# Turning the first norm's result in 32 by 32 blocks on VectorE, with tokens in another order, instead of on TensorE

## The chip, the cores and the metric

One core of a Trainium2 chip. The metric is the device time of one execution of the whole program, in microseconds (us). The engines are named as the profile names them: PE (TensorE), DVE (VectorE), ACT (ScalarE), POOL (GpSimd) and SP (SyncE, which here only issues DMAs).

## What is computed

One decoder layer over 16 sequences of 512 tokens with 256 features, float32 throughout. Cut to what matters here:

```python
x = layernorm(x + attention(x))      # 16 heads of 16, causal, rope, LoRA on q and v
x = layernorm(x + ffn(x))            # first norm's result goes into the FFN
# ffn: h = gelu(butterfly(x @ W_exp + b_exp) + up_bias)      1024 hidden units
#      y = butterfly(h) @ W_con + b_con + down_bias
```

Both butterflies are linear and are folded into the two weight matrices at the start of the program, so that the FFN is two matrix products with a gelu between them. The first, the expansion, needs the first norm's result with features on the partitions; the norm makes it with tokens on the partitions. So each sequence's 512 by 256 result has to be turned.

## The kernel before

**Slots.** The program is an order written out by hand. A sequence is 20 slots long (`per`), four quads of 5 slots each (two feature chunks by two head parities). In each slot PE makes one share of the score products twice: once for the row maxima of the present quad (`largest`, L407, tile `pa` in most slots) and once for the softmax weights of the quad three quads, 15 slots, behind (`weights`, L457, tile `pb`). DVE reads the first for the maxima (L426, `junk`), ACT takes the exponential of the second (L488), POOL zeroes the masked half of the diagonal blocks (L492). `pa` and `pb` are one buffer each, so that the scores of a slot wait until DVE and ACT have read those of the slot before. Then `weigh` (L506) multiplies the weights with v (`po`, L516), and after it come the tasks of the slot's list `others[s]`, in the order of their `add` calls, and last those of `holes[s]`. Each engine takes its own instructions in this order; SP does so with the DMAs, and a DMA that has to wait holds all DMAs behind it on SP.

**The tail of a sequence.** The numbers below count slots from the sequence's first; slot 40 + n is slot n of the sequence two later, so that these tasks are the fillers between that sequence's score products. In slots 40 to 42 the attention's output is projected and added to x in tile `z` (L589, L601), `spread`, `offset` and `centre` (L616, L628, L635) make the first norm in place on `z`, the last of them on ACT in slot 44. In slot 45 `turn_x1` (L647) runs for both feature chunks: four PE transposes of 128 by 128 each into a PSUM bank, one DVE copy of the bank into `x1T` (L653); POOL then adds the output bias to `z` (L657). In slots 46 to 49 `hidden` (L664) makes the expansion's eight chunks of 128 hidden units, two in a slot (`ph`; a chunk is 8 products in the code, two feature halves by four column groups of 32, and 16 matmuls in the profile), and DVE or ACT copies each out (L680, L682). In slot 50 ACT applies the gelu. From slot 51 `contract` (L691) makes the second product (`py`, L81 in `columns`), one token tile of 128 in two halves, each half one task; the last token tile's halves stand in slots 63 and 64, which are slots 43 and 44 of the next sequence. `spread`, `offset`, `centre` and `store` make the second norm in slots 65 to 68.

**Other tasks there.** `project_v` (L380) of the sequence two later has one of its four tiles in slot 42. The heads' scales take a chain of their own through SP: `normalize_heads` (L533) stores the sums and moves the odd rows (L546, L550) in slot 45, `gather` (L554) loads the sums as `few`, DVE inverts them (`invert`, L561), SP stores them (`recips`), repeats them (`wide`) and loads them (`spread`), and POOL multiplies with them in slots 49 and 50 (`scale`, L577).

The last two sequences have an order of their own: sequence 14's turn stands in slot 46, its expansion from slot 47 on, one chunk in a slot; sequence 15 is turned at the very end. A pool of three PSUM banks, `ps_w`, serves `ph`, `py`, `pvv`, `pwo` and `pt`.

Of the kernel before, what the change touches and what calls it, by code (L numbers as in the profile page):

```python
# [11 lines left out]
F32 = mybir.dt.float32  # L12
BF16 = mybir.dt.bfloat16
AF = mybir.ActivationFunctionType
ALU = mybir.AluOpType
PSUM = bass.MemoryType.PSUM

P = 128
NH = 16
DH = 16  # L20
HG = 32
NG = P // HG
# [11 lines left out]
def decoder_layer(  # L34
# [18 lines left out]
    nc = tc.nc  # L53
    B, T, D = x.shape
    NT = T // P
    NC = D // P
    DHID = wcon.shape[0]
    NHC = DHID // P
# [5 lines left out]
    ring2 = ctx.enter_context(tc.tile_pool(name="ring2", bufs=2))  # L64
# [3 lines left out]
    dram = ctx.enter_context(tc.tile_pool(name="dram", bufs=4, space=bass.MemoryType.DRAM))  # L68
# [5 lines left out]
    def bank(name, shape):  # L74
        return ps_w.tile(shape, F32, tag="w", name=name)

    def columns(out, w, moving, start, stop):

        for g in range(NG):
            part = slice(HG * g, HG * (g + 1))  # L80
            nc.tensor.matmul(out[part, :], w[:, part], moving, start=start, stop=stop)  # L81
# [10 lines left out]
    xTs, zs = {}, {}  # L92
# [23 lines left out]
    wdn = const.tile([P, NHC, D], F32, name="wdn")  # L116
    bias2 = const.tile([P, 2, D], F32, name="bias2")
# [337 lines left out]
    state = {}  # L455
# [151 lines left out]
    def stats_of(which, b, t):  # L607
        if t == 0:
            state["stats", which, b] = small.tile(
                [P, NT, 2], F32, tag=f"stats{which}", name=f"stats{which}_{b}"  # L610
            )
        bn = small.tile([P, nc.vector.BN_STATS_DIM], F32, tag="bn", name=f"bn{which}_{b}_{t}")
        nc.vector.bn_stats(bn, zs[b][:, t, :])
        nc.vector.bn_aggr(state["stats", which, b][:, t, :], bn)
# [13 lines left out]
    def offset(which, b, t0=0, t1=NT):  # L628
        stats, norm = state["stats", which, b], state["norm", which, b]
        ts = slice(t0, t1)  # L630
        nc.vector.scalar_tensor_tensor(  # L631
            norm[:, 2, ts], stats[:, ts, 0], -1.0, norm[:, 1, ts], ALU.mult, ALU.mult
        )
# [10 lines left out]
            )  # L644


    def turn_x1(b, c):  # L647
        if c == 0:
            state["x1T", b] = ring2.tile([P, NC, T], F32, tag="x1T", name=f"x1T_{b}", bufs=1)
        pt = bank(f"pt1_{b}_{c}", [P, NT, P])  # L650
        for t in range(NT):
            nc.tensor.transpose(pt[:, t, :], zs[b][:, t, c * P : (c + 1) * P], ident)  # L652
        nc.vector.tensor_copy(  # L653
            state["x1T", b][:, c, :], pt.rearrange("p t q -> p (t q)")
        )
        if c == NC - 1:
            nc.gpsimd.tensor_tensor(  # L657
                zs[b],
                zs[b],
                bias2[:, 0:1, :].to_broadcast([P, NT, D]),  # L660
                ALU.add,
            )

    def hidden(b, hc, fused=False):  # L664
        if hc == 0:
            state["h", b] = hpool.tile([P, NHC, T], F32, tag="h", name=f"h_{b}")
        ph = bank(f"ph_{b}_{hc}", [P, T])
        for c in range(NC):
            columns(
                ph,  # L670
                wup[:, c, hc * P : (hc + 1) * P],
                state["x1T", b][:, c, :],
                c == 0,
                c == NC - 1,
            )
        h = state["h", b][:, hc, :]
        if fused:
            nc.scalar.activation(h, ph, AF.Gelu, bias=hbias[:, hc : hc + 1])  # L678
        elif hc % 4 == 0:
            nc.vector.tensor_copy(h, ph)  # L680
        else:
            nc.scalar.copy(h, ph)  # L682

    def gelus(b, count=NHC):
        h = state["h", b]
        for hc in range(count):
            nc.scalar.activation(  # L687
                h[:, hc, :], h[:, hc, :], AF.Gelu, bias=hbias[:, hc : hc + 1]
            )

    def contract(b, t, half):  # L691
        if half == 0:
            state["py"] = bank(f"py_{b}_{t}", [P, D])
        py = state["py"]
        for hc in range(half * NHC // 2, (half + 1) * NHC // 2):
            columns(
                py,
                state["h", b][:, hc, t * P : (t + 1) * P],
                wdn[:, hc, :],
                hc == 0,  # L700
                hc == NHC - 1,
            )
        if half == 1:
            nc.vector.tensor_add(zs[b][:, t, :], py, zs[b][:, t, :])  # L704
            stats_of(2, b, t)

    def store(b):
        nc.sync.dma_start(out[b].rearrange("(t p) d -> p t d", p=P), zs[b])
# [14 lines left out]
    end = B * per + behind  # L723
# [6 lines left out]
    def add(s, f, *args):  # L730
        others[s].append(lambda: f(*args))

    def start_projection(b, side, c):
        state["pr", b, side, c] = project(b, side, c)
# [13 lines left out]
    for b in range(B):  # L748
        s = b * per
        if b > 0:  # L750

            at = {1: (-16, -11, -13, -9), B - 1: (-3, 2, 10, 10)}.get(b, (-3, -1, 2, 12))
            for t in range(NT):
                add(s + at[t], project_v, b, t)
        if b + 1 < B:

            add(s - head * (b == 0), load_xT, b + 1)
            at = {0: (2, 5, 7, 10), 1: (3, 6, 8, 11)}.get(b, (10, 10, 10, 10))
            for i, (c, side) in enumerate(chains):
                holes.setdefault(s + at[i], []).append(  # L760
                    lambda b=b, side=side, c=c: start_projection(b + 1, side, c)
                )
                turning = s + max(at[0] + 1 + 3 * i, at[i] + 1)
                for step in range(3):
                    add(turning + step, turn, b + 1, side, c, step)
                for step in range(1 + side):
                    add(turning + (6 if i == 3 else 4) + step, part, b + 1, side, c, step)
        add(s + 9, load_x, b)
        add(s + 11, place_largest, b, 0)
        add(s + 21, place_largest, b, 1)  # L770
        for c in range(NC if b + 1 < B else 1):
            if c + 1 < NC:
                add(s + 25 + (b + 1 == B), gather, b, c)
            add(s + (26, 36)[c] + (b + 1 == B), invert, b, c)
            for t in range(NT):
                add(s + ((29, 29, 30, 30), (39, 39, 40, 40))[c][t], scale, b, c, t)
        if b + 1 < B:
            for t in range(NT):
                add(s + (40, 40, 41, 41)[t], project_out, b, t)
                add(s + (40, 40, 41, 42)[t], add_attention, b, t)  # L780
            add(s + 42, spread, 1, b)
            others[s + 43].insert(0, lambda b=b: offset(1, b))
            add(s + 44, centre, 1, b)
            for c in range(NC):
                add(s + 45 + (b + 2 == B), turn_x1, b, c)
        if b + 2 < B:

            late = 2 * (b + 3 == B)
            for hc in range(NHC - late):
                add(s + 46 + hc // 2, hidden, b, hc)  # L790
            holes.setdefault(s + 50, []).insert(0, lambda b=b, late=late: gelus(b, NHC - late))
            for hc in range(NHC - late, NHC):
                holes[s + 50].append(lambda b=b, hc=hc: hidden(b, hc, True))
            for t in range(NT):
                for half in range(2):
                    at = (11, 13, 14, 15, 16, 18, 23, 24)[2 * t + half]
                    if b + 3 == B and t == NT - 1:
                        at = (23, 25)[half]
                    add(s + 40 + at, contract, b, t, half)
            add(s + 65, spread, 2, b)  # L800
            add(s + 67, offset, 2, b)
            add(s + 68, centre, 2, b)
            add(s + 68, store, b)
# [3 lines left out]
    y, z = B - 2, B - 1  # L807
# [4 lines left out]
    for hc, at in ((3, 10), (4, 10), (5, 10), (6, 11), (7, 11)):  # L812
        add(edge + at, hidden, y, hc, True)

    add(end - 3, contract, y, 0, 0)
    add(end - 1, contract, y, 0, 1)
    add(end + 2, contract, y, 1, 0)
    add(end + 2, contract, y, 1, 1)
    for t in range(NT):
        add(end + 2, normalize, z, NC - 1, t)  # L820
    add(end + 2, contract, y, 2, 0)
    for t in range(NT + 1):
        if t < NT:
            add(end + 3, project_out, z, t)
# [2 lines left out]
        if t > 0:  # L827
            add(end + 3, offset, 1, z, t - 1, t)
            add(end + 3, centre, 1, z, t - 1, t)
    add(end + 3, contract, y, 2, 1)  # L830
    add(end + 3, contract, y, 3, 0)
    for c in range(NC):
        add(end + 5, turn_x1, z, c)
    add(end + 5, contract, y, 3, 1)
    for hc in range(NHC):
        add(end + 5, hidden, z, hc, True)
    add(end + 5, spread, 2, y)
# [2 lines left out]
    add(end + 6, store, y)  # L840
    for t in range(NT):
        for half in range(2):
            add(end + 7, contract, z, t, half)
        add(end + 7, finish_tile, z, t)


    first, second = fold_tasks()
# [180 lines left out]
```

## Time and profile before

| what | value |
|---|---|
| device time, median of 3 runs | 1315.29 us (1312.11 to 1317.72) |
| the profiled execution's own time | 1318.97 us |
| its span, first to last instruction | 1317.0 us, so 1.97 us lie around it |
| DVE busy | 780.5 us (59%) |
| ACT busy | 702.9 us (53%) |
| POOL busy | 565.1 us (43%) |
| DVE copies of the turned blocks (L653) | 32, 678 ns each |
| POOL bias add (L657) | 16, 2381 ns each |
| mean share of the 16 DMA engines, by queue | 16.0% and 1.4% for the two that SP and ACT issue to |
| HBM traffic | 40.17 MB read, 18.06 MB written |

A row of the profile that counts a group of instructions reads: line, engine, operation, output from inputs, shape, count, then busy time and the mean duration of one, and after the second bar how long the engine stood idle before them and who ended the wait. Matmuls overlap, so a group's busy time is less than its count times its mean.

### The profile page before, as it was taken

To read this page: it belongs to the slowest core of one execution; us is meant where nothing else is said; L and a number is where in the kernel's file an instruction comes from. 1 tells how busy PE (TensorE), PEld (TensorE's weight loads), DVE (VectorE), ACT (ScalarE), POOL (GpSimd) and SP (SyncE) were. 2 spreads that over 40 slices of the span, in tenths; PEclk is the share of its full clock that TensorE was granted. 3 is DMA by queue.
4 is the path that set the end of the run, shared out by engine and by line. 5 is a ranking of instruction groups with operands and counts; after the bars stand their busy time and mean duration, and the time that the engine had idled before them with its cause. 6 is when DMAs were issued, how large, how long until landed. Compare 5 with 4: busy or idle time off the path is not lost.

```text
span 1317.0 us, 38318 instructions
## 1 busy us (share of the span) xinstructions
PE 1280.6 (97%) x15896; PEld 575.2 (44%) x15896; DVE 780.5 (59%) x2760; ACT 702.9 (53%) x1047; POOL 565.1 (43%) x905
## 2 busy tenths in 40 slices
PE   8888999999999999999999999999999999999998
PEld 3343435444353544435354443535444353444443
DVE  5776746657465665747566574756657474665431
ACT  2574455555646555564655546465555646455643
POOL 4525325445362544536254453625445362532430
PEclk9889999999999999999999999999999999999999
DMA  5411111111212111121211112121211212111101
GB/s 169 132 32 59 40 49 46 56 56 41 82 41 65 47 56 56 41 83 41 69 42 57 56 41 83 41 67 45 56 56 40 83 41 70 41 40 32 43 20 34
DMA packets 64062, 74.07 MB, mean 56 GB/s; under 512 B 23120, under 2 KB 42576, under 8 KB 63888
## 3 DMA queue, kind: packets, MB, share of 16 engines
q1 hardware_dynamic: 60000, 66.07, 16.0%
q10 hardware_dynamic: 3888, 5.55, 1.4%
q8 instruction: 125, 2.05, 0.7%
q14 instruction: 49, 0.40, 0.1%
HBM read 40.17 MB, written 18.06 MB: 44 GB/s over the span
## 4 chain that ended last, share of the span: by engine, by line
PE 92%; DVE 3%; ACT 2%; DMA 1%; issue 1%; POOL 0%; SPq 0%; POOLq 0%; DVEq 0%; ACTq 0%
PE pb L474 21%; PE py L81 17%; PE ph L81 16%; PE po L516 12%; PE pqk L81 8%; PE pa L417 4%; PE pwo L81 4%; PE pvv L81 4%; DVE junk L426 1%; PE pd L81 1%; PE pt L652 1%; PE pa L474 1%; PE pb L417 1%; ACT pT L488 1%; ACT h L687 0%
## 5 line engine op out<-in xcount | busy, mean ns | idle before, releaser
L426 DVE CUSTOM_DVE_ANT_0 junk<-pa,causal 128x384 bf16<-128x384 f32 (+2 forms) x878 | 438.6, 500 | 339.0 <-PE pa L417 271.6
L488 ACT ACTIVATE pT<-pb 128x1024 f32<-128x1024 f32 (+1 forms) x314 | 294.2, 937 | 354.8 <-PE pa L417 183.8
L492 POOL TENSOR_SCALAR_AFFINE_SELECT pT<-pT 128x256 f32<-128x256 f32 x512 | 202.3, 407 | 651.4 <-ACT pT L488 650.4
L474 PE MATMUL pb<-qz,kz 17*128 17x512 f32 (+2 forms) x1756 | 330.9, 475 | 17.6 <-ACT pT L488 11.7
L417 PE MATMUL pa<-kz,qz 32*128 32x384 f32 (+3 forms) x1756 | 330.6, 476 | 3.4 <-DVE mx L426 3.4
L81 PE MATMUL py<-wdn,h 128*32 128x256 f32 x4096 | 244.3, 381 | 0.0
L81 PE MATMUL ph<-x1T,yb 128*32 128x512 f32 x2048 | 231.6, 594 | 0.2 <-ACT h L678 0.2
L474 PEld LDWEIGHTS pb<-qz,kz 17*128 17x128 f32 (+1 forms) x1756 | 142.4, 184 | 196.4 <-issue 92.3
L516 PE MATMUL po<-pT,vaug 128*32 128x512 f32 (+3 forms) x2048 | 180.9, 447 | 1.8 <-POOL pT L492 1.8
L81 PEld LDWEIGHTS py<-wdn,h 128*32 128x32 f32 x4096 | 125.3, 110 | 99.2 <-issue 12.7
L417 PEld LDWEIGHTS pa<-kz,qz 32*128 32x128 f32 (+1 forms) x1756 | 143.2, 185 | 14.6 <-DVE mx L426 11.6
L81 PEld LDWEIGHTS ph<-x1T,yb 128*32 128x32 f32 x2048 | 63.2, 110 | 139.8 <-issue 107.6
L81 PE MATMUL pqk<-xT,wqk 128*32 128x512 f32 x1024 | 117.6, 608 | 0.0
L682 ACT COPY h<-ph 128x512 f32<-128x512 f32 x84 | 49.2, 585 | 117.3 <-PE ph L81 117.2
L516 PEld LDWEIGHTS po<-pT,vaug 128*32 128x32 f32 x2048 | 47.9, 109 | 105.3 <-issue 59.1
L426 DVE DVE_READ_ACCUMULATOR2_ANT mx<- 128x1 f32 x1024 | 84.6, 83 | 0.0
L638 ACT ACTIVATE z<-z,norm 128x256 f32<-128x256 f32 x128 | 66.7, 589 | 23.2 <-DVE norm L631 23.2
L365 POOL TENSOR_TENSOR swap<-swap,rope_sb 128x512 f32<-128x512 f32 x62 | 78.8, 1270 | 0.0
L426 DVE CUSTOM_DVE_ANT_0 junk<-pb,causal 128x256 bf16<-128x256 f32 (+3 forms) x146 | 63.6, 436 | 16.4 <-PE pb L417 2.5
L687 ACT ACTIVATE h<-h,hbias 128x512 f32<-128x512 f32 x113 | 70.8, 709 | 0.2
L704 DVE TENSOR_TENSOR z<-py,z 128x256 f32<-128x256 f32 x64 | 27.2, 425 | 72.9 <-PE py L81 70.6
L81 PE MATMUL pvv<-wv_sb,xT 128*32 128x256 f32 x1024 | 66.5, 379 | 0.0
(91 smaller groups left out, 1192.1 us busy)
## 6 DMA issues: line engine op xcount, KB each, us to landing
xT<-in_xT SPq DMA_DIRECT2D x16, 512.0 KB
swap<-qz SPq DMA_DIRECT2D x64, 128.0 KB
swap<-kz SPq DMA_DIRECT2D x64, 128.0 KB
z<-in_x SPq DMA_DIRECT2D x16, 512.0 KB
wide<-recips SPq DMA_DIRECT2D x31, 256.0 KB
spread<-wide SPq DMA_DIRECT2D x31, 256.0 KB
out_y<-z SPq DMA_DIRECT2D x15, 512.0 KB
x<-x SPq DMA_DIRECT2D x32, 128.0 KB
```

The lines of the kernel that those rows point to most:

```text
L81: nc.tensor.matmul(out[part, :], w[:, part], moving, start=start, stop=stop)
L365: engine.tensor_tensor(swap, swap, rope_sb[:, 1, :], ALU.mult)
L417: lambda i=i, rows=rows, at=at, n=n, t=t, ps=ps: nc.tensor.matmul(ps[:, i, at : at + n], q[rows, par, t * P : n], k_[rows, par, 0:n], star ...
L426: lambda i=i, at=at, n=n, t=t, g=g, ps=ps: nc.vector.tensor_tensor_reduce(out=junk[:, 0:n], in0=ps[:, i, at : at + n], in1=causal[:, T - n ...
L474: lambda i=i, rows=rows, at=at, n=n, k=block, ps=ps: nc.tensor.matmul(ps[:, i, at : at + n], kt[rows, par, k * P : (k + 1) * P], qt[rows, ...
L488: nc.scalar.activation(pT[:, heads, 0:n], ps[:, :, at : at + n], AF.Exp)
L492: nc.gpsimd.affine_select(out=diag, in_=diag, pattern=[[0, 2], [1, P]], compare_op=ALU.is_ge, fill=0.0, base=0, channel_multiplier=-1,)
L516: nc.tensor.matmul(po[HG * g : HG * (g + 1), k * P : T], vaugs[b % 2][:, k, NG * c + g, first : first + HG], pT[:, g, at : at + n], start= ...
L638: nc.scalar.activation(zs[b][:, t, :], zs[b][:, t, :], AF.Identity, bias=norm[:, 2, t : t + 1], scale=norm[:, 1, t : t + 1],)
L682: nc.scalar.copy(h, ph)
L687: nc.scalar.activation(h[:, hc, :], h[:, hc, :], AF.Gelu, bias=hbias[:, hc : hc + 1])
L704: nc.vector.tensor_add(zs[b][:, t, :], py, zs[b][:, t, :])
```

## The change

For sequences 0 to 14 the PE transposes are gone. `turn_blocks`, called in slot 45, turns the four token tiles of `z` on DVE in one instruction, in blocks of 32 by 32: block k of 32 features of all four token tiles comes to lie on 32 partitions each. Four DMAs on SP, one for each group g of 32 partitions, write these to a DRAM tensor `x1rows` (128 KB each, rows of 512 bytes), and a fifth (512 KB, rows of 2 KB) loads `x1T` from it. In `x1T` the tokens then have the order (g, t, i), where token = 128 t + 32 g + i. The order is carried through `hidden` and the gelu, and `contract` undoes it by the columns of `h` that it takes as the stationary operand; sequence 15, which still has `turn_x1`, keeps the plain order. The two DVE copies of a sequence go as well.

Around it: the expansion begins in slot 47 with three chunks in a slot (sequence 13: two, without those that are already fused with the gelu); `project_v`'s third tile moves from slot 42 to slot 46 for sequences 2 to 14; the last token tile's contraction is cut into four quarters in slots 62 to 65 (slots 42 to 45 of the next sequence) instead of two halves in 63 and 64, except for sequence 13; the second norm's `spread` goes from slot 65 to 66, again except for sequence 13. For sequence 14 the turn moves from slot 46 to 45. In the program's order on SP the five new DMAs stand behind the odd rows' move (L550 of the kernel before) and ahead of the load of `few`.

```diff
+    def turn_blocks(b):
+        state["x1T", b] = ring2.tile([P, NC, T], F32, tag="x1T", name=f"x1T_{b}", bufs=1)
+        turned = ring2.tile([P, D // HG, NT, HG], F32, tag="turned", name=f"turned_{b}", bufs=1)
+        nc.vector.transpose(turned, zs[b].rearrange("p t (k j) -> p k t j", j=HG))
+        rows = dram.tile([D, NG, P], F32, tag="x1rows", name=f"x1rows_{b}")
+        for g in range(NG):
+            nc.sync.dma_start(
+                rows.rearrange("(k j) g q -> j k g q", j=HG)[:, :, g, :],
+                turned[HG * g : HG * (g + 1)].rearrange("j k t i -> j k (t i)"),
+            )
+        nc.sync.dma_start(state["x1T", b], rows.rearrange("(c p) g q -> p c (g q)", p=P))
+        nc.gpsimd.tensor_tensor(
+            zs[b],
+            zs[b],
+            bias2[:, 0:1, :].to_broadcast([P, NT, D]),
+            ALU.add,
+        )
...
-    def contract(b, t, half):
+    def contract(b, t, first, past):
...
+            of = h.rearrange("p c (g t i) -> p c t g i", g=NG, i=HG)
+        for hc in range(first, past):
+            for g in range(NG):
+                nc.tensor.matmul(
+                    py[HG * g : HG * (g + 1), :],
+                    of[:, hc, t, g, :],
+                    wdn[:, hc, :],
...
-            at = {1: (-16, -11, -13, -9), B - 1: (-3, 2, 10, 10)}.get(b, (-3, -1, 2, 12))
+            at = {1: (-16, -11, -13, -9), B - 1: (-3, 2, 10, 10)}.get(b, (-3, -1, 6, 12))
...
-            for c in range(NC):
-                add(s + 45 + (b + 2 == B), turn_x1, b, c)
+            add(s + 45, turn_blocks, b)
...
-                add(s + 46 + hc // 2, hidden, b, hc)
+                add(s + 47 + hc // (2 if late else 3), hidden, b, hc)
...
+                for n in range(4):
+                    add(s + 62 + n, contract, b, NT - 1, 2 * n, 2 * n + 2)
+            add(s + 65 + (b + 3 < B), spread, 2, b)
```

More of the change, by code (lines that the diff above doesn't have):

```diff
@@ L689, in gelus, with halves @@
             )
-    def contract(b, t, half):
-        if half == 0:
+    def contract(b, t, first, past):
+        if first == 0:
             state["py"] = bank(f"py_{b}_{t}", [P, D])
         py = state["py"]
[L695 to L703, printed above, removed]
+        h = state["h", b]
+        if b + 1 == B:
+            of = h.rearrange("p c (t g i) -> p c t g i", g=NG, i=HG)
+        else:
+            of = h.rearrange("p c (g t i) -> p c t g i", g=NG, i=HG)
[5 more added lines that the diff above has]
+                    wdn[:, hc, :],
+                    start=(hc == 0),
+                    stop=(hc == NHC - 1),
+                )
+        if past == NHC:
             nc.vector.tensor_add(zs[b][:, t, :], py, zs[b][:, t, :])
             stats_of(2, b, t)
+    def halves(b, t, half):
+        contract(b, t, half * NHC // 2, (half + 1) * NHC // 2)
     def store(b):
@@ L793, in decoder_layer @@
                 holes[s + 50].append(lambda b=b, hc=hc: hidden(b, hc, True))
-            for t in range(NT):
+            for t in range(NT - 1):
                 for half in range(2):
[L796 to L800, printed above, removed]
+                    add(s + 40 + (11, 13, 14, 15, 16, 18)[2 * t + half], halves, b, t, half)
+            if b + 3 == B:
+                for half in range(2):
+                    add(s + (63, 65)[half], halves, b, NT - 1, half)
+            else:
+                for n in range(4):
+                    add(s + 62 + n, contract, b, NT - 1, 2 * n, 2 * n + 2)
+            add(s + 65 + (b + 3 < B), spread, 2, b)
             add(s + 67, offset, 2, b)
@@ L813, in decoder_layer @@
         add(edge + at, hidden, y, hc, True)
[L815 to L818, printed above, removed]
+    add(end - 3, halves, y, 0, 0)
+    add(end - 1, halves, y, 0, 1)
+    add(end + 2, halves, y, 1, 0)
+    add(end + 2, halves, y, 1, 1)
     for t in range(NT):
         add(end + 2, normalize, z, NC - 1, t)
-    add(end + 2, contract, y, 2, 0)
+    add(end + 2, halves, y, 2, 0)
     for t in range(NT + 1):
@@ L829, in decoder_layer @@
             add(end + 3, centre, 1, z, t - 1, t)
-    add(end + 3, contract, y, 2, 1)
-    add(end + 3, contract, y, 3, 0)
+    add(end + 3, halves, y, 2, 1)
+    add(end + 3, halves, y, 3, 0)
     for c in range(NC):
         add(end + 5, turn_x1, z, c)
-    add(end + 5, contract, y, 3, 1)
+    add(end + 5, halves, y, 3, 1)
     for hc in range(NHC):
@@ L842, in decoder_layer @@
         for half in range(2):
-            add(end + 7, contract, z, t, half)
+            add(end + 7, halves, z, t, half)
         add(end + 7, finish_tile, z, t)
```

## The prediction, made before the changed kernel ran

> **What bounds the kernel now.** I read the page first: busy shares, then the chain that ended last, then the rows of what is removed.
>
> ```profile
> PE 1280.6 (97%) x15896; PEld 575.2 (44%) x15896; DVE 780.5 (59%) x2760; ACT 702.9 (53%) x1047; POOL 565.1 (43%) x905
> ...
> PE 92%; DVE 3%; ACT 2%; DMA 1%; issue 1%; POOL 0%; SPq 0%; POOLq 0%; DVEq 0%; ACTq 0%
> ...
> L652 PE MATMUL pt<-ident,z 128*128 128x128 f32 x128 | 17.6, 280 | 0.0
> ```
>
> PE is the bound almost throughout, so a microsecond off PE is worth a microsecond, if nothing else comes late in its place. All 16 turns keep PE busy 17.6 us; 15 go. So the gain has a ceiling of about 15 x 1.1 = 16 us, and the question is whether the replacement arrives in time. For that I read the chain in order of time (start, us, what) over slots 45 to 47 of one sequence in mid-run:
>
> ```profile
> 627.67 0.63 PE pb L474 x2
> ...
> 628.74 0.57 PE po L516 x8
> 629.31 1.02 PE pt L652 x8
> 630.33 0.63 PE pb L474 x2
> ...
> 631.45 3.57 PE ph L81 x32
> 635.02 0.52 PE pb L474 x2
> ...
> 636.10 1.00 PE po L516 x8
> 637.10 3.43 PE ph L81 x32
> 640.53 0.52 PE pb L474 x2
> ```
>
> Slots begin at 627.67, 630.33, 635.02 and 640.53. The turn holds the chain for 1.02 us, and the expansion starts 2.14 us after the turn's start. The products `ph` are the long fillers here: while PE makes them, DVE and ACT catch up on the scores. Next, DVE and SP in the same stretch, from the timeline:
>
> ```profile
> 629.57 0.69 DVE L426 CUSTOM_DVE_ANT_0 junk<-pa,causal 128x512 bf16<-128x512 f32 x1
> ...
> 630.28 1.27 DVE L653 COPY x1T<-pt 128x512 f32<-128x512 f32 x2
> ```
>
> ```profile
> 631.00 0.53 SPq L550 DMA_DIRECT2D x<-x  x1
> 632.08 0.32 SPq L558 DMA_DIRECT2D few<-sums  x1
> 634.35 0.33 SPq L566 DMA_DIRECT2D recips<-few  x1
> 635.81 0.62 SPq L569 DMA_DIRECT2D wide<-recips  x1
> 638.87 0.32 SPq L574 DMA_DIRECT2D spread<-wide  x1
> ```
>
> The two maxima of a slot with 512 columns take DVE about 1.43 us (628.83 to 630.26). SP shows what a trip by way of DRAM costs: `spread` cannot issue until `wide` has landed, 3.06 us after `wide` was issued (256 KB); `recips` to `wide` is 1.46 us (16 KB).
>
> **The change, part by part, for this sequence.**
>
> *Removed.* PE's 1.02 us and DVE's 1.27 us.
>
> *Slots 42 to 45.* Slots 43 and 44 each lose half of a 1.73 us `py` task. Slot 43 gets nothing from it: the scores of slot 44 start at 623.74 because DVE reads slot 43's until 623.67. I charge 1.0 us for that. The other 0.75 us is kept, so slot 45 begins at about 626.9 instead of 627.67. There PE makes scores (1.07), `po` (0.57) and a `py` quarter (0.87), until 629.4. The quarter ends the token tile, so DVE adds it and takes statistics (0.42 + 0.43 + 0.18, with gaps 1.09) until 630.55, and only then turns.
>
> *The DVE turn.* No row has this shape. A turn of 128x32 takes 193 ns (L444); the two copies of 512 columns each (1024 in all) took 1.27 us. Bounds: 0.7 us (a copy of half the columns) and 2.4 us (POOL's pass over 128x1024). I take 1.25 us by the copies, which have its element count. It ends at T = 631.8.
>
> [...]
>
> *The five DMAs.* None is in the trace. Two-part issues of 128 KB (`swap`) follow each other by 0.51 to 0.56 us, so the fourth write is issued at T + 1.7. A 128 KB issue's last packet ended 1.7 us after its start (655.40 to 657.11), and SP goes on 0.37 us after a landing: the load of `x1T` is issued at T + 3.75. The 512 KB load of `xT` ended 3.47 us after issue, that of `z` 3.66 us: T + 7.2, and PE starts at about T + 7.4 = 639.2. From below: issues 0.41 us apart (0.33 as for `rows`), a landing in 1.06 us, the load in 3.3: T + 6.2. From above: the last write as slow as `wide` (3.06) and the load as slow as `z`: T + 8.9.
>
> *When PE wants `x1T`.* Slot 46 now holds only scores and one `pvv` task (0.86 us), until 631.45. Behind the turn on DVE wait slot 46's maxima (631.8 to 633.25), so slot 47's `pa` products wait until 633.25: about 1.35 us of PE idle. POOL's bias add (2.38 us) now follows the turn too, until 634.2, and slot 46's masking (0.41) is behind it: `po` of slot 47 loses another 0.6 us and ends at 635.2. PE then stands at `ph` until 639.2: **4.0 us**.
>
> *What else is behind these waits.* On SP, `few` is issued only after the `x1T` load, and its packets come behind it. DVE waits for `few` at L564 with slot 47's maxima behind it, until about 639.5; `ph` covers that (three chunks, 5.2 us). `spread` lands about 6 us later than now, near 647, while POOL wants it in slot 49, which now begins at about 650: covered, by 3 us; if not, POOL's masks and then `po` wait for the rest.
>
> *Sum.* Slot 47 now ends at 640.53 with four chunks made. After: 639.2 + 7.0 us for four chunks = 646.2. That is **+5.7 us a sequence**: the terms, -1.02 for the turn and +1.0, +1.35, +0.6 and +4.0 for the waits, add to 5.9; I keep the count to slot 47's end. The other chunks and the `py` quarters keep their length. Sequences 0, 13 and 14 have other fillers but the same trip by way of DRAM; I count them alike: 15 x 5.7 = 85 us.
>
> *The clock.* A stretch of nearly 8 us (631.45 to 639.2) would have PE busy for some 1.8 us. What the clock does then, the windows show near the start (stretch, its length, PE, PEld, DVE, ACT, POOL busy, then the granted clock):
>
> ```profile
> 123.20:126.60 3.40, 0.85 (x8) 0.30 (x4) 3.26 (x11) 1.02 (x1) 2.29 (x3) 1.00 0.14 49
> 126.60:133.50 6.90, 6.83 (x52) 3.13 (x52) 2.54 (x12) 3.23 (x7) 2.17 (x4) 0.51 0.01 2
> ...
> 160.80:164.20 3.40, 2.67 (x34) 1.55 (x32) 2.77 (x11) 1.02 (x1) 1.15 (x3) 1.00 0.02 5
> 164.20:167.70 3.50, 3.50 (x24) 1.74 (x28) 2.40 (x9) 3.13 (x6) 0.81 (x2) 0.51 0.00 0
> ```
>
> After 3.4 us with PE 0.85 us busy the clock was halved for 6.9 us, and once for 3.5 us after a much busier stretch. The new stall is as idle as the first of these. Half clock for 3.4 to 6.9 us, part of it still inside the wait, costs 0 to 3.4 us a sequence; I take 1.9: 15 x 1.9 = 28 us.
>
> [...]
>
> **The rivals.**
>
> *Stall without the clock.* The same waits, but the clock holds: 1319 + 85 = 1404, by the median 1400. For it: near 1196 us PE idled 1.4 us at a time and the clock stayed at 1.0. Against it: the first window above.
>
> *Mostly hidden.* The trip takes as little as about 4 us, so that only the DVE and POOL waits stay: (-1.02 + 2.9) x 15 = 28, so 1343. For it: the queue is nearly empty here (41 to 70 GB/s in most slices). Against it: `rows` to the maxima's landing, the smallest such pair, takes 3.75 us without 512 KB to move.
>
> *Not slower.* The mechanism is PE's own lag at slot 47. If the other engines run ahead, so that T comes about 3 us earlier against PE (the turn needs only ACT's `centre`, done at 628.48, and the `py` quarter's statistics) and the writes land quickly, then PE meets `x1T` ready, and 1.02 us a sequence is gained: 1319 - 15 = 1304, by the median 1300. It decides when all waits together stay under 1.02 us. Against it: slots 45 and 46 without long fillers leave PE no lag.
>
> *Worse still.* The late `spread` outlasts its 3 us of cover under a slow trip: 2 to 4 us more a sequence, about 1465.
>
> **How the numbers follow.** Likeliest, at 0.57, is the stall with the halved clock: 1319 + 85 + 28 = 1432 against the profile's own 1319; the median of the runs lies 3.7 us lower, so **1428**. Stall without the clock 0.26, mostly hidden 0.08, not slower 0.04, worse still 0.05. The low end, 1375, is the trip and turn at their lower bounds with the clock held (15 x 4.0 = 60); the high end, 1465, lies 2.5 us a sequence above the forecast, and the upper bounds together would go beyond it. Half a per cent, about 6.6 us, is what a measurement of this kernel can tell from no change: faster 0.04, within it 0.02, slower 0.94.
>
> **What would show it.** In the changed profile, the PE load for `ph` should wait on the DMA `x1T` some 4 us at a time, 15 times; slot 47's `pa` should wait for DVE; the turn should show about 1.25 us; L564's wait for `few` should rise from 13.6 us in all to over 50; PEclk should show digits under 9 in mid-run. If the waits on `x1T` are under 1 us, the DMA step is wrong; if the clock stays at 0.99, the clock step is. I would be wrong outright if PE reached slot 47 later than 635 for a reason that does not lengthen the program.

## The result, and the profile after

The changed kernel takes 1443.05 us in the median of six runs (1440.29 to 1446.99), against 1316.45 us before; the ratio is 1.0971, with a 95% interval of 1.0945 to 1.0997. The forecast was 1428 us in a range of 1375 to 1465. The profiled execution took 1445.02 us, its span is 1443.3 us.

The page of the kernel after: busy shares, the granted clock in tenths, the chain by engine, the expansion's products, and DVE's inversion of `few`.

```profile
PE 1327.3 (92%) x15776; PEld 576.1 (40%) x15776; DVE 790.7 (55%) x2745; ACT 699.3 (48%) x1047; POOL 563.8 (39%) x905
...
PEclk9998999999999999999998989999899999989899
...
PE 76%; DVE 9%; DMA 8%; ACT 3%; issue 2%; SPq 2%; POOL 0%; DVEq 0%; POOLq 0%; ACTq 0%
...
L81 PE MATMUL ph<-x1T,yb 128*32 128x512 f32 x2048 | 258.6, 656 | 61.6 <-DMA x1T<-x1rows 61.4
...
L564 DVE RECIPROCAL few<-few 128x32 f32<-128x32 f32 x31 | 10.9, 353 | 99.3 <-DMA few<-sums 99.2
```

PE's share of the chain fell from 92% to 76%; DVE and the DMAs took what it lost. PE now stands 61.4 us in all for `x1T`. The time in which PE is not busy (span less busy time) grew from 36.4 to 116.0 us, and PE is also busy 46.7 us longer, with 120 matmuls fewer. The clock digits drop to 8 in mid-run; on the page of before they stay at 9 there:

```profile
PEclk9889999999999999999999999999999999999999
```

The chain in order of time for the sequence ahead of the one in the prediction, whose slots are filled alike (slot 45 begins at 591.12 here; start, us, what), shows each link of the trip:

```profile
591.12 0.70 PE pb L474 x2
...
592.94 0.91 PE py L721 x16
...
594.97 1.26 DVE turned L651
...
597.63 2.46 DMA x1rows<-turned
...
600.23 3.60 DMA x1T<-x1rows
...
603.87 7.80 PE ph L81 x48
611.67 0.52 PE pb L474 x2
```

Quarter, statistics, turn, writes, load, expansion: from 592.94 to 603.87 the chain is never on PE's score products. SP in that stretch, from the timeline:

```profile
596.25 1.85 SPq L654 DMA_DIRECT2D x1rows<-turned  x4
600.23 0.38 SPq L658 DMA_DIRECT2D x1T<-x1rows  x1
600.71 0.41 SPq L558 DMA_DIRECT2D few<-sums  x1
604.45 0.33 SPq L566 DMA_DIRECT2D recips<-few  x1
```

The four issues take 1.85 us, SP waits until 600.23 for the writes to land, and only then can `few` go.

The windows around the wait (stretch, its length, PE, PEld, DVE, ACT, POOL busy, then the granted clock, DMA share, GB/s):

```profile
598.60:602.01 3.41, 1.52 (x12) 0.29 (x8) 0.08 (x1) 1.02 (x1) 2.13 (x5) 1.00 0.51 103
602.01:608.84 6.83, 4.97 (x24) 1.17 (x28) 2.71 (x11) 0.00 (x0) 0.00 (x0) 0.50 0.34 107
```

PE was busy 1.52 us of 3.41, then the clock was halved for 6.83 us, 4.97 us of them with PE at work. That is why three expansion chunks took 7.80 us where 5.15 us were due (three times half of the 3.43 us that two took before).

### The profile page after: what moved, and what is told of

It reads as the page before. It is cut to its first block, busy times and chain, and to the rows that moved or that the text cites. A ratio compares the mean times of both kernels' runs of the same rounds, so it can differ in the third digit from the quotient of the medians.

```text
span 1443.3 us, 38171 instructions
## 1 busy us (share of the span) xinstructions
PE 1327.3 (92%) x15776; PEld 576.1 (40%) x15776; DVE 790.7 (55%) x2745; ACT 699.3 (48%) x1047; POOL 563.8 (39%) x905
## 4 chain that ended last, share of the span: by engine, by line
PE 76%; DVE 9%; DMA 8%; ACT 3%; issue 2%; SPq 2%; POOL 0%; DVEq 0%; POOLq 0%; ACTq 0%
PE ph L81 17%; PE pb L474 15%; PE py L721 14%; PE po L516 9%; PE pqk L81 8%; DVE junk L426 4%; PE pa L417 4%; DMA x1T<-x1rows 4%; PE pwo L81 4%; DMA x1rows<-turned 3%; PE pvv L81 3%; SPq L654 1%; ACT pT L488 1%; DVE turned L651 1%; PE pa L474 1%
## 5 line engine op out<-in xcount | busy, mean ns | idle before, releaser
L81 PE MATMUL ph<-x1T,yb 128*32 128x512 f32 x2048 | 258.6, 656 | 61.6 <-DMA x1T<-x1rows 61.4
L721 PE MATMUL py<-wdn,h 128*32 128x256 f32 x4096 | 249.1, 381 | 0.0
L516 PE MATMUL po<-pT,vaug 128*32 128x512 f32 (+3 forms) x2048 | 189.3, 454 | 1.8 <-POOL pT L492 1.8
L81 PEld LDWEIGHTS ph<-x1T,yb 128*32 128x32 f32 x2048 | 67.9, 119 | 230.8 <-issue 147.2
L564 DVE RECIPROCAL few<-few 128x32 f32<-128x32 f32 x31 | 10.9, 353 | 99.3 <-DMA few<-sums 99.2
```

The costliest lines, as they stand in the source:

```text
L516: nc.tensor.matmul(po[HG * g : HG * (g + 1), k * P : T], vaugs[b % 2][:, k, NG * c + g, first : first + HG], pT[:, g, at : at + n], start= ...
L721: nc.tensor.matmul(py[HG * g : HG * (g + 1), :], of[:, hc, t, g, :], wdn[:, hc, :], start=(hc == 0), stop=(hc == NHC - 1),)
```

## The experiments

Every kernel ran next to the kernel before on the same chip. One table first; ratios against the kernel before, with their 95% intervals:

| run | median us | ratio | clock in the profiled run |
|---|---|---|---|
| e1_moves | 1347.07 | 1.0223 (1.0204 to 1.0242) | 0.985 |
| e2_nowait | 1376.24 | 1.0446 (1.0420 to 1.0472) | 0.983 |
| e3_warm | 1425.01 | 1.0818 (1.0780 to 1.0856) | 0.987 |
| e4_turn | 1466.60 | 1.1142 (1.1122 to 1.1161) | 0.942 |
| e5_few | 1448.53 | 1.0995 (1.0966 to 1.1025) | 0.955 |
| e6_nowait_few | 1352.67 | 1.0266 (1.0236 to 1.0296) | 0.989 |
| e7_cover | 1323.45 | 1.0047 (1.0026 to 1.0067) | 0.993 |
| e8_cover_pe | 1329.04 | 1.0078 (1.0052 to 1.0105) | 0.989 |
| e9_few_between | 1319.44 | 1.0007 (0.9989 to 1.0025) | 0.989 |
| e10_early | 1325.68 | 1.0057 (1.0038 to 1.0077) | 0.989 |
| e11_invert | 1315.56 | 0.9980 (0.9963 to 0.9997) | 0.993 |
| e12_shift | 1315.08 | 0.9991 (0.9973 to 1.0009) | 0.994 |

The kernel before has a clock of 0.989 in its profiled run, the changed kernel 0.960.

The theory was the prediction's: waits for `x1T`, small waits for DVE and POOL in slots left without long fillers, and a halved clock (the expectations call its sum of these terms the ledger). The rivals were that the moves are harmless, that DVE's wait for `few` does the damage, and that the clock does not matter.

### The two halves of the change by themselves

**e1_moves**: the turn stays on PE, and with it the plain order of tokens; everything else as in the change.

```diff
-            add(s + 45, turn_blocks, b)
+            for c in range(NC):
+                add(s + 45, turn_x1, b, c)
```

> The moves alone: the turn stays on TensorE (slot 45), the expansion begins in slot 47 and the fillers stand where the change puts them. Theory of the ledger: 1.0 us wait behind slot 43 and about 1.35 us for the maxima behind the DVE copies, a sequence, no trip by way of DRAM and no halved clock: 15 x 2.4 = 35, so about 1350. Rival, the moves cost nothing and all loss is the trip: 1316 to 1322.

Measured 1347, 30 us over the kernel before. The moves have a price of their own with no trip at all. PE's weight loads and matmuls for `pa` wait 23.5 and 7.6 us for DVE's maxima in the profile, against 11.6 and 3.4 us before. That is not all of it: PE is also busy 19.8 us longer (1300.4 us against 1280.6), and by the trace's records the score products, `pa` and `pb` together, cover 418.5 us of the span instead of 402.2. The waits for `pa` before, and then in e1_moves:

```profile
PEld pa L417 <- DVE mx L426: 11.6, 19, 2.1
```

```profile
PEld pa L417 <- DVE mx L426: 23.5, 43, 1.9
```

**e4_turn**: the turn and its trip, all fillers where they were before, `project_v`'s third tile too.

```diff
...
-            add(s + 45, turn_blocks, b)
+            add(s + 45 + (b + 2 == B), turn_blocks, b)
...
-                add(s + 47 + hc // (2 if late else 3), hidden, b, hc)
+                add(s + 46 + hc // 2, hidden, b, hc)
...
+            for t in range(NT):
+                for half in range(2):
+                    at = (11, 13, 14, 15, 16, 18, 23, 24)[2 * t + half]
...
+                    add(s + 40 + at, halves, b, t, half)
```

> The turn alone: block turn and trip, but the expansion from slot 46 and all fillers where they were before. Theory: PE stands at the first expansion chunk in slot 46 for about 7.7 us instead of the several waits, net 7.7 us a sequence and at least as much clock: 15 x 7.7 + 15 x 2.5 = 150, about 1465. Rival, the moves are the larger part of the loss: below 1400.

Measured 1467. The wait for `x1T` is 120.9 us in all, 8.1 us a sequence where 7.7 were expected, and the mean clock falls to 0.942. So the moves of the change are worth their 30 us: the whole loss is 150 us without them and 127 with them.

### The wait, `few`, and the clock

**e2_nowait**: a weight tile in place of `x1T`.

```diff
-                state["x1T", b][:, c, :],
+                (state["x1T", b] if b + 1 == B else wqk)[:, c, :],
```

> The changed kernel, but the expansion of sequences 0 to 14 takes a weight tile of the same shape that lies in SBUF from the start in place of x1T (so it computes something else); the block turn and its five DMAs still run. Theory of the ledger: the 4.0 us wait and the halved clock go, the small waits stay, and DVE's wait for few now shows for up to 0.9 us: 15 x (1.7 to 2.6), 1342 to 1356, clock back at 0.99. Rival, that it is DVE's wait for few, with the maxima queued behind it, that holds PE: above 1400, since that wait is still there.

Measured 1376, above the theory's 1342 to 1356 and below the rival's 1400: neither. The wait for `x1T` and what hangs on it are worth 67 us of the 127, but more was left than I had counted.

**e6_nowait_few**: the same, with `few` loaded ahead of the turn's DMAs.

```diff
-                add(s + 25 + (b + 1 == B), gather, b, c)
+                if b + 1 < B:
+                    others[s + 25].insert(0, lambda b=b, c=c: gather(b, c))
+                else:
+                    add(s + 26, gather, b, c)
```

> As e2_nowait (the expansion of sequences 0 to 14 takes a weight tile in place of x1T), and the load of few ahead of the turn's DMAs. Theory: without the wait for x1T the late few is bare, 0.9 us a sequence; with it gone 15 x 0.9 = 13 less than e2_nowait, about 1363, near e1_moves less the PE turns. Rival, few costs nothing here either: 1376.

Measured 1353: the late `few`, once bare, costs 23.6 us (1376.24 less 1352.67), not 13. That is what the sum for e2_nowait had left out. In e2_nowait DVE waits 97.0 us in all for it, here 16.3. One part of the expectation does not come out: e1_moves less the PE turns would be about 1332, and this run is 20 us above that. PE's loads and matmuls for `pa` wait 38.3 and 16.7 us for DVE's maxima here, against 23.5 and 7.6 us in e1_moves. What of the turn on DVE, the bias add behind it and the five DMAs holds DVE up was not tried apart.

**e5_few**: this order of `few` alone, with the wait for `x1T` left in.

> The changed kernel with one order undone: the load of few stands on SP ahead of the five DMAs of the turn again. DVE's wait for few should fall from 99 us in all to about 15. Theory: PE stands at the expansion for x1T during that wait anyway, so the time stays, 1438 to 1446. Rival, that the late few (and the maxima behind it on DVE) is a cost of its own: 13 us or more less, 1430 or below.

Measured 1449, a little above the expected range, its interval overlapping that of the changed kernel. DVE's wait for `few` is down to 15.1 us, as expected, and PE's wait for `x1T` is about what it was (61.4 us in the changed kernel):

```profile
PE ph L81 <- DMA x1T<-x1rows: 60.0, 15, 7.2
...
DVE few L564 <- DMA few<-sums: 15.1, 12, 9.2
```

The 99 us that DVE stands at `few` in the changed kernel are covered: PE stands for `x1T` at the same time. A long wait in the list of waits cost nothing here, and 23.6 us as soon as the wait above it was gone. With `few` early in both, e5_few and e6_nowait_few differ by the wait for `x1T` alone: the wait and the clock that goes with it are worth 96 us (1448.53 less 1352.67), where the prediction had 15 x 4.0 + 28 = 88.

**e3_warm**: idle products ahead of the first expansion chunk.

```diff
+            if b + 1 < B:
+                fill = bank(f"fill_{b}", [P, D])
+                for n in range(3):
+                    for c in range(NC):
+                        columns(fill, wqk[:, c, n * P : (n + 1) * P], wv_sb[:, c, :], n + c == 0, n + c == 3)
```

> The changed kernel with 2.6 us of idle products on TensorE (48 matmuls of 256 columns on weights, result not used) ahead of the first expansion chunk of sequences 0 to 14, more work for the bound engine. Theory that the stall halves the clock and that this costs 2.1 us a sequence: the products lie inside the 3.7 us wait, the clock stays up, 15 x 2.1 = 32 less, about 1411. Rival, the clock is not driven by this wait or costs nothing: 1443 or, where the products outlast the wait, up to 1460.

Measured 1425: TensorE has 39 us more work to do (15 x 2.6; 32 products of this size took 1.73 us in the kernel before, so 48 take 2.6), and the program is 18 us shorter. The direction is the theory's, the size is 14 us short of it. Its four runs are 1417.64, 1424.38, 1425.63 and 1430.17 us, at mean clocks of 0.987, 0.979, 0.983 and 0.975: by and large the lower the clock, the longer the run, from the first to the last some 10 us for each 0.01. The changed kernel's runs have 0.957 to 0.966. So the products do not keep the clock up in every execution; where they did best, the run is 25 us under the changed kernel's median. What remains of the wait for `x1T` in the profiled run, the first of the four, is 24.1 us on the matmuls, 1.6 us a sequence: the products take 37 us off the wait, about what they add. So what is gained must be the clock's. Counted in that trace's records PE is busy 32 us at half clock, against 89 us in the changed kernel; half of the difference is 28 us, and the run is 27 us shorter than the profiled run of the changed kernel.

### A cover that fits

**e7_cover** puts work that exists anyway into the gap: the projections of a later sequence. Sequences 13 and 14 turn on PE again, and `few` goes first on SP. The cut shows the new places against the kernel before:

```diff
+                early = at if b < 2 else (5, 6, 6, 7)
-                holes.setdefault(s + at[i], []).append(
+                holes.setdefault(s + early[i], []).append(
...
-            late = 2 * (b + 3 == B)
+            late = 2 if b + 3 == B else 4
             for hc in range(NHC - late):
-                add(s + 46 + hc // 2, hidden, b, hc)
+                add(s + (46 if b + 3 == B else 48) + hc // 2, hidden, b, hc)
```

> Another cover for the trip: block turn for sequences 0 to 12 with few first on SP, fillers of before, but the query and key projections of the sequence three later (6.9 us of products) come in slots 45 to 47 instead of 50, and the expansion in slots 48 to 50, its last four chunks fused with the gelu. Theory: x1T lands about when PE gets there, the wait and the halved clock go, and 13 x 1.02 = 13 us of PE turns are gained: 1300 to 1312. Rival, another wait takes its place (the gelus without the projections as cover, the swaps behind the trip on SP, DVE): 1320 to 1350.

Measured 1323, in the rival's range. 120 us of the loss are gone, but not all of it. In its profile PE still waits 7.2 us on the matmuls and 9.3 us on the weight loads for `x1T`, up to 1.6 us at a time: `few`, put first, waits on SP for its own sums and delays the writes. Around 632 us the writes begin 0.97 us after the odd rows' move there, and 0.11 us after it in e9_few_between.

**e8_cover_pe** is the same order with the turn on PE.

> The order of e7_cover with the turn on TensorE, no trip. If the block turn buys the PE time of the turns and nothing else, this is 13 us slower than e7_cover. If the order alone has its price, it shows here against the kernel before: theory 1312 to 1322, rival above 1330.

Measured 1329, between the two ranges: the order alone costs 12 us against the kernel before, and the block turn in it is 5.6 us better than the PE turn (the intervals of the two ratios overlap a little, 1.0026 to 1.0067 against 1.0052 to 1.0105, so that this is not quite clear of the noise), less than the 13 us of PE time that it saves.

**e9_few_between** issues `few` between the four writes and the load of `x1T`.

> e7_cover with the load of few between the four writes and the load of x1T on SP, where SP waits for the writes anyway. In e7_cover SP issued few first and the writes 0.9 us late, and PE stood up to 1.2 to 1.4 us at the expansion. Theory: that wait nearly goes, 13 x 0.9 = 12 less than e7_cover's 1323, about 1312. Rival, the wait is not what separates e7_cover from the kernel before (its gelus without cover are): 1321 to 1324.

Measured 1319, the same as the kernel before: 4 us less than e7_cover where 12 were expected, and below the rival's range too. No wait of PE for `x1T` is left in the list, but its place was taken. The timeline of DVE in e9_few_between:

```profile
639.16 0.35 DVE L564 RECIPROCAL few<-few 128x32 f32<-128x32 f32 x1 [3.97 <-DMA few<-sums]
...
640.57 0.55 DVE L426 CUSTOM_DVE_ANT_0 junk<-pa,causal 128x384 bf16<-128x384 f32 x1
```

DVE stands 3.97 us for `few`, which SP issued at 635.38, right behind the four writes, and slot 47's maxima come after it.

**e11_invert** moves the inversion one slot on.

```diff
-            add(s + (26, 36)[c] + (b + 1 == B), invert, b, c)
+            add(s + (26 + (0 < b < B - 2), 36)[c] + (b + 1 == B), invert, b, c)
```

> e9_few_between with the inversion of few (L564) one slot later for sequences 1 to 13, behind slot 47's maxima on DVE. In e9_few_between the wait for x1T was gone, but DVE stood up to 4.0 us at few, whose load came behind the four writes, and slot 47's maxima and so the scores of slot 48 stood behind it. Theory: with that wait out of the way about 1 us a sequence more is gained, 1303 to 1310, under the kernel before. Rival, the next thing is as late (x1T lands at about the same time, ACT's gelus in slot 50): 1314 to 1320.

Measured 1315.56, ratio 0.9980 (0.9963 to 0.9997): under the kernel before by 0.2%, just clear of its interval, short of the 1303 to 1310 expected and in the rival's range. DVE's and PE's waits there in e9_few_between, and then in e11_invert:

```profile
DVE few L564 <- DMA few<-sums: 45.5, 27, 4.0
...
PEld pa L417 <- DVE mx L426: 15.6, 22, 2.1
```

```profile
PEld pa L417 <- DVE mx L426: 10.9, 16, 2.1
...
DVE few L564 <- DMA few<-sums: 5.0, 12, 1.1
```

DVE's wait fell by 40 us, PE's by 5 and the time by 4: most of DVE's wait had been covered. A short wait of PE for `x1T` is back, 2.8 us on the matmuls and 4.0 on the loads.

**e10_early** and **e12_shift** are two attempts to spread this better: the turn and its writes already in slot 44 with the fourth projection back in slot 50, and the third projection a slot later.

> As e9_few_between, and the block turn with its writes already in slot 44, right behind the centring, the load of x1T in slot 45 as before; the fourth projection goes back to slot 50 behind the gelus, as cover. Theory: x1T lands about 2 us earlier, no wait for it is left and slot 50 loses its gap, so what the PE turns cost is gained: 1300 to 1310. Rival, the turn ahead of slot 45's maxima on DVE holds the scores of slot 46: 1315 to 1325.

> As e11_invert, with the third projection in slot 47 instead of 46, so that DVE's copies spread more evenly over the trip. Theory: within 3 us of e11_invert, since the cover in all is the same. Rival, slot 46 with one filler less lets DVE hold the scores of slot 47: 8 us more or above.

e10_early took 1326, just past the upper end of its rival's range: the turn ahead of slot 45's maxima is no gain. PE's loads for `pa` wait 19.6 us for DVE's maxima, against 15.6 in e9_few_between, which fits the rival, but which of its two moves costs the time was not tried apart. e12_shift took 1315, the same as e11_invert; its ratio is not clear of 1.

## Why the prediction was right, point by point

- **The turn on DVE.** Taken at 1.25 us, measured 1.246 us in the mean of 15 (128x1024, float32; 1.239 to 1.248). The block turn loses in this kernel by the price of its trip (in e4_turn PE waits 8.1 us a sequence for `x1T`) and not by its own time.
- **The trip.** In the sequence shown the turn ends at T = 596.22. The load of `x1T` is issued at T + 4.0 (forecast T + 3.75), PE starts at T + 7.65 (forecast T + 7.4).
- **The wait for `x1T`.** Forecast 4.0 us a sequence, measured 61.4 us over 15, 4.1 us. PE was ready at T + 3.9 in this sequence, 0.5 us later than forecast, so that the two slips nearly cancel: that the wait came out this close is partly luck.
- **The small waits.** Forecast 1.0 + 1.35 us for the moves alone; e1_moves shows 30 us instead of 35. All the terms but the wait for `x1T`, 1.9 us a sequence or 29 us, are what e6_nowait_few has left: 35 us over the kernel before. Slot 45 began 5.1 us before T, against 4.9 forecast.
- **`few`.** It was forecast to be covered, and e5_few shows that it is. Its bare price was set at 0.9 us a sequence in the expectations and is 1.6 us (e6_nowait_few against e2_nowait, 23.6 / 15). The late `spread` was covered too: PE's loads for `po` wait 11.4 us in all behind POOL's product with it, 12.1 us before.
- **The clock.** Forecast 28 us. Counted in the trace's records, PE was busy 89 us at half clock, against 25.5 us before; half of the difference is 32 us. That half of the time is lost fits the sequence shown, where PE was at work for 4.97 us at half clock and the three chunks took 2.65 us longer than due. e3_warm shows that work put into the wait brings 18 us of it back in the median; in its profiled run, the best one, it brings 27 us where the count gives 28. The rest, to 32, is from the trace's count alone. The forecast had the stall as the cause. In eleven sequences the clock was halved during the wait for `x1T` or right after it; in the other four it was halved before that wait began (see the last section), so that there the wait is not what set it off.
- **The sum.** Forecast 113 us, measured 126.6. Of the 13.6 us, about 4 lie in the clock by the trace's count. The other 10 us are 0.6 us a sequence. In the sequence shown, slots 40 to 47 and the fourth chunk take 8.8 us more than before (575.26 to 611.67 and 1.76 us for the chunk, a third of the 5.29 us that slot 48's three take, against 611.20 to 640.53); 2.65 of that is the expansion at half clock, which leaves 6.2 where the ledger had 5.7. This half microsecond is spread over the terms: about 0.15 ahead of slot 45, 0.2 from there to T, 0.25 in the trip, and 0.1 less in the chunks. The last 0.1 us I have not placed. PE is busy longer than the clock and the missing turns explain, by some 31 us over the program. About half of it is there in e1_moves too, where the score products overlap less; that they do so because their pairs wait for DVE is my reading and was not tried.

The rival that ended on the other side needed T about 3 us earlier against PE. e7_cover to e11_invert show the other way to the same end, PE 4 us later with useful work, and what it brings when it is reached: 0.2% at most, where 13 turns take 1.0% on PE. The order takes the rest: by itself it costs 12 us (e8_cover_pe). Against e8_cover_pe, e11_invert is 1.0% better (0.9980 against 1.0078), about what the turns take, though the two also differ in the place of `few` and its inversion.

## What to carry to other kernels

When work leaves the bound engine, look first at what the bound engine will do while the replacement is under way: on PE the block was turned, copied and in use 2.1 us after the turn began, while the trip by way of DRAM, with two dependent transfers, took 7.65 us from the end of the turn to the first product. A wait that shows long in the list can be free today and the next one to bite: DVE's wait for `few` cost nothing until the wait over it was gone. And the cover should be work that the program has anyway, in slots where the other engines' reads are not held up by it; test the new order with the old operation, as e8_cover_pe does, before giving the operation the credit.

## What the runs showed of the hardware that was not expected

The clock was halved after stretches that were far from idle. In the changed kernel (columns as above):

```profile
765.85:769.26 3.41, 2.71 (x28) 1.14 (x20) 3.06 (x6) 1.65 (x4) 2.69 (x3) 1.00 0.65 151
769.26:779.50 10.24, 7.33 (x36) 1.57 (x36) 2.70 (x11) 0.70 (x1) 1.73 (x4) 0.50 0.36 94
```

PE was busy for 2.71 of 3.41 us, the wait for `x1T` began only at 771.25, and yet the clock was halved from 769.26 on, for 10.24 us. It is one of four such sequences: in each the halving came before the wait for `x1T`, after a stretch of 3.41 us with PE busy for 2.19 to 2.71 us. Over the 15 sequences it was halved for 3.41 us eight times, 6.83 us twice and 10.24 us five times. The prediction put the halving down to the stall; in the stretch shown PE idles for 0.70 us in all, and the halving came ahead of a wait of 2.91 us. What sets it off is not shown by these runs: in the kernel before, a window with less PE time than this one went by at full clock, and so did the next:

```profile
1195.11:1198.52 3.41, 2.00 (x32) 0.90 (x27) 0.55 (x4) 2.10 (x3) 0.41 (x1) 1.00 0.05 7
1198.52:1201.94 3.42, 3.24 (x40) 1.47 (x36) 2.04 (x11) 1.56 (x2) 0.77 (x2) 1.00 0.02 2
```
